# A graph layer's last places, its last blocks of nodes and its normalization, arranged differently

## The chip, the core and the metric

The kernel runs on one core of a Trainium2 chip. A core has five engines with instruction streams of their own: TensorE (PE in the profile; its weight loads are PEld), VectorE (DVE), ScalarE (ACT), GpSimd (POOL) and SyncE (SP), which here only issues DMAs. They wait for one another through semaphores, and each works its own instructions off in order. Sixteen DMA engines move data between the device memory and the on-chip memory. The metric is the time of one execution on the device, in microseconds (us).

## The reference

A message-passing layer over 12,500 nodes with 128 features and 400,000 edges sorted by destination, followed by a layer normalization over the features:

```
rbf      = exp(-(distances[:, None] - centers)**2 / (2 * width * width))      # 50 centers
cut      = 0.5 * (cos(pi * distances / 10) + 1) * (distances <= 10)
W        = (silu(rbf @ fw1 + fb1) @ fw2 + fb2) * cut[:, None]
messages = (h[src] @ pw + pb) * W
agg      = segment_sum(messages, dst, num_segments=num_atoms)
h_new    = h + (silu(agg @ mw1 + mb1) @ mw2 + mb2)
out      = layernorm(x + h_new)                                               # h is x
```

Edges longer than 10 have a factor of zero. The lengths are drawn so that 71,145 of the 400,000 edges are kept.

## The kernel before

**Preparation.** The projection h @ pw + pb of all nodes is computed first and stored in device memory as `proj`, 12,500 rows of 512 bytes. The edge list is taken in five chunks. For each, `pack` throws out the long edges by shifts and predicated copies on VectorE, and writes what is left close together into `packed`, a list in device memory that is cleared to zero beforehand. One entry has the source node (14 bits), the destination (14 bits) and a bit 28 that is set for an edge and not for an empty place. `pack` then reads the packed list back (`two`, L405), takes the source out of it (`part`, L408), clips it to N - 1 (`f_src`, L411), and turns it through TensorE into `srci`, the row indices of the gathers (L421). The list has 141 x 512 = 72,192 places. Places that no edge fills are zero, so that their source is row 0; their factor `cut` is zero.

**The loop.** It goes over 141 quads (`NQ`), each of four times 128 places. `fetch(q + 3)` (L478) issues four gathers on GpSimd, each of 128 rows of `proj` into `got`; `got` has eight buffers. `first` and `tanh`/`silu` compute the inner layer for two quads together, `second` (L539) the outer one into `pu` on TensorE, `message` (L550) multiplies `pu` by `got` on VectorE, `place` (L555) builds one-hot matrices `hot` of the edges' destinations on VectorE, `sum_up` (L564) adds up on TensorE into `pa`, and `add` (L583) adds `pa` at a place read from a register into `aggT` on VectorE. `add(q - 1)` stands behind `message(q)` and `place(q + 1)`. The schedule is manual: each engine runs its instructions in the order in which the program has them.

**The nodes.** The rows of nodes are worked off in 25 blocks of four tiles of 128 (the last has two: 128 and 84 rows), named by their first tile: 0, 4, ... 96. `node_first` (L594) has two matmuls on TensorE out of `aggT` and a tanh on ScalarE, `node_silu` (L604) one operation on VectorE, `node_second` (L611) nine matmuls on TensorE, then on VectorE one addition of 2x and four `bn_stats`. `scales` (L623) takes the statistics of up to four blocks and works out the reciprocal root by Newton steps on tiny tiles on VectorE, 20 operations, twelve of them in the four steps. `normalize` (L652) has one ScalarE activation for each tile and a store on SyncE.

As destinations are sorted, a block can begin when the quads with its destinations have been added. The lines L698 to L706 give each block a quad at which it begins in the loop, three quads apart and behind a bound on the progress of the list (`done_to`); the loop is left when a block would begin at quad 139 or later. So blocks 0 to 84 are in the loop (84 begins at 136), and 88, 92 and 96 are left to `finish` behind the last add. `nodes(q)` (L708) is called at the head of each quad; it has at most one block to normalize, and the stage of the block whose turn it is. At quad 137 it issues the loads of x for all blocks that are left. `finish` (L671) runs the rest, takes all their statistics in one group, and normalizes.

Of the kernel before, what the change touches and what calls it, by code (L numbers as in the profile page):

```python
# [10 lines left out]
F32 = mybir.dt.float32  # L11
BF16 = mybir.dt.bfloat16
I32 = mybir.dt.int32
AF = mybir.ActivationFunctionType
OP = mybir.AluOpType
# [13 lines left out]
SB = 14  # L29
# [5 lines left out]
NC_ = len(QB) - 1  # L35
NQ = QB[-1]
# [9 lines left out]
def kernel(  # L46
# [37 lines left out]
    nc = tc.nc  # L84
    N, H = x.shape
# [14 lines left out]
    x_sb = {}  # L100

    def load_x(t0, name="x4", bufs=8):
        t = work.tile([P, 4, H], F32, name=name, bufs=bufs)
        node_dma(t0, t, x, False)
        x_sb[t0] = t
# [88 lines left out]
    for name in ("pb", "fb2", "mb1", "mb2"):  # L194
# [4 lines left out]
    iota_n = keep.tile([P, WS], F32, name="iota_n")  # L199
# [23 lines left out]
                            op0=OP.mult, op1=OP.mult)  # L223
# [33 lines left out]
    for c in range(NC_):  # L257
        nc.vector.tensor_scalar(lim[:, c:c + 1], part_f[:64], float(2 * QB[c] - DONE[1]), 0.0,
                                op0=OP.add, op1=OP.max)
# [33 lines left out]
    def pack(c):  # L293

        if c + 1 < NC_:
# [12 lines left out]
                                op0=OP.mult, op1=OP.add)  # L308
# [9 lines left out]
        else:  # L318
# [14 lines left out]
        nodes = rowed(I32, "nodes", bufs=2)  # L333
        nc.vector.scalar_tensor_tensor(nodes, rel, SB, r_src, op0=OP.logical_shift_left,
                                       op1=OP.bitwise_or)
        yield 0.7
        nc.vector.scalar_tensor_tensor(nodes, step, LB, nodes, op0=OP.logical_shift_left,
                                       op1=OP.bitwise_or)
        yield 0.7
        for b in range(bits):  # L340
            k = 1 << b
# [4 lines left out]
                                    op0=OP.logical_shift_left, op1=OP.arith_shift_right)  # L346
            yield 0.4
            m = go[:, k:n + k]
            if b < bits - 1:
# [3 lines left out]
                                               op1=OP.bitwise_and)  # L353
                yield 0.7
                nc.vector.copy_predicated(after[:, :n], m, nodes[:, k:n + k])  # L355
                nodes = after
            else:
# [8 lines left out]
                                op1=OP.bitwise_and)  # L366
        nc.vector.tensor_scalar(to, to, first, None, op0=OP.add)
        yield 0.4
        both = rowed(I32, "both", CAP)
        nc.vector.tensor_scalar(both, front, (1 << SB) - 1, SB, op0=OP.bitwise_and,  # L370
                                op1=OP.logical_shift_left)
# [4 lines left out]
                                op0=OP.is_lt, op1=OP.mult)  # L376
        line = work.tile([P, CAP, 2], I32, name="line", bufs=2)
        nc.vector.scalar_tensor_tensor(line[:, :, 0], both, 1 << 2 * SB, there,
                                       op0=OP.bitwise_or, op1=OP.bitwise_and)
# [11 lines left out]
        p0, np_ = 2 * QB[c], 2 * (QB[c + 1] - QB[c])  # L391
# [5 lines left out]
        def paired(dt, name):  # L397
# [6 lines left out]
        two = paired(I32, "two")  # L404
        nc.vector.tensor_tensor(two, pair[:np_, 0, ::2], pair[:np_, 1, ::2], OP.bitwise_or)  # L405
        yield 0.7
        part = paired(I32, "part")
        nc.vector.tensor_scalar(part, two, SB, (1 << SB) - 1, op0=OP.logical_shift_right,  # L408
                                op1=OP.bitwise_and)
        f_src = paired(F32, "f_src")  # L410
        nc.vector.tensor_scalar(f_src, part, float(N - 1), None, op0=OP.min)  # L411
        yield 0.4
        tp = bank("ms").rearrange("p (f j e) -> p f j e", f=4, j=2)

# [7 lines left out]
        part = paired(I32, "part")  # L422
# [152 lines left out]
    def base_of(q, ks=(0, 1)):  # L575
        for k in ks:
            _, v = nc.values_load_multi_w_load_instructions(  # L577
                base_i[0:1, 2 * q + k:2 * q + k + 1], engines=[mybir.EngineType.DVE],
                min_val=0, max_val=N - W,
                skip_runtime_bounds_check_because="bases are destinations, and at most N - W")  # L580
            bases[q, k] = v[0]

    def add(q):  # L583
        pa = pa_of.pop(q)
        for k in range(2):
            to = aggT[:, ds(bases.pop((q, k)), W)]
            nc.vector.tensor_add(to, to, pa[:, k * W:(k + 1) * W])  # L587
# [6 lines left out]
    def node_first(t0):  # L594

        n = sum(rows(t0))
        pz = bank("ms")
        nc.tensor.matmul(pz[:, :n], bias_b["mb1"][:, 0, :], ones_b[:, :n], start=True, stop=False)
        nc.tensor.matmul(pz[:, :n], mw1_sb, aggT[:, t0 * P:t0 * P + n], start=False, stop=True)  # L599
        t = work.tile([P, QE], F32, name="zt", tag="xT", bufs=3)  # L600
        nc.scalar.activation(t[:, :n], pz[:, :n], AF.Tanh, scale=0.5)  # L601
        z_of[t0] = pz, t

    def node_silu(t0):  # L604
        n = sum(rows(t0))
        pz, t = z_of.pop(t0)
        s = work.tile([P, QE], F32, name="zs", tag="hp", bufs=3)
        nc.vector.scalar_tensor_tensor(s[:, :n], t[:, :n], 1.0, pz[:, :n], op0=OP.add, op1=OP.mult)
        zs_of[t0] = s

    def node_second(t0, st, tag="pu"):  # L611

        r = rows(t0)
        y = x_sb[t0]
        py = bank(tag).rearrange("p (k f) -> p k f", k=4)
        rows_times(py, zs_of.pop(t0), late["mw2"], bias_b["mb2"], r)
        for a, c, m in alike(r):
            nc.vector.scalar_tensor_tensor(y[:m, a:a + c], y[:m, a:a + c], 2.0, py[:m, a:a + c],
                                           op0=OP.mult, op1=OP.add)
        for k, m in enumerate(r):  # L620
            nc.vector.bn_stats(st[:m, k, :], y[:m, k, :])

    def scales(st, n):  # L623


        def tmp(name, dt=F32):
            return work.tile([P, 16], dt, name=name, bufs=1)[:, :n]

        def sts(o, a, v, b, op0, op1):
            nc.vector.scalar_tensor_tensor(o, a, v, b, op0=op0, op1=op1)  # L630

        mean, dif, v = tmp("mean"), tmp("dif"), tmp("v")
        nc.vector.tensor_add(mean, st[:, :n, 1], st[:, :n, 4])
        nc.vector.tensor_sub(dif, st[:, :n, 1], st[:, :n, 4])
        sts(dif, dif, 0.25, dif, OP.mult, OP.mult)
        nc.vector.tensor_add(v, st[:, :n, 2], st[:, :n, 5])
        sts(v, v, 1.0 / H, dif, OP.mult, OP.add)
        nc.vector.tensor_scalar(v, v, LN_EPS, None, op0=OP.add)
        g_i, g, w = tmp("g_i", I32), tmp("g"), tmp("w")
        nc.vector.tensor_scalar(g_i, v.bitcast(I32), 1, None, op0=OP.logical_shift_right)  # L640
        nc.vector.tensor_scalar(g_i, g_i, -1.0, float(0x5f3759df), op0=OP.mult, op1=OP.add)
        r, by = (work.tile([P, 16], F32, name=k, bufs=2)[:, :n] for k in ("rs", "by"))
        a = g_i.bitcast(F32)
        for k in range(4):
            nc.vector.tensor_mul(g, a, a)
            sts(w, g, -0.5, v, OP.mult, OP.mult)
            sts(r, w, 1.5, a, OP.add, OP.mult)
            a = r
        sts(by, mean, -0.5, r, OP.mult, OP.mult)
        return r, by  # L650

    def normalize(t0, rs, by):  # L652
        y = x_sb.pop(t0)
        for k, m in enumerate(rows(t0)):
            nc.scalar.activation(y[:m, k, :], y[:m, k, :], AF.Identity, bias=by[:m, k:k + 1],  # L655
                                 scale=rs[:m, k:k + 1])
        node_dma(t0, y, out, True)

    ready = []
# [1 line left out]
    def scaled(group, st):  # L661

        rs, by = scales(st, sum(len(rows(t)) for t in group))
        ready.extend((t, rs[:, t - group[0]:], by[:, t - group[0]:]) for t in group)
# [3 lines left out]
        nc.vector.memset(st, 0.0)  # L668
        return st

    def finish(these):  # L671

        for t0 in these[:4]:
            if t0 not in x_sb:
                load_x(t0)
        node_first(these[0])
        node_silu(these[0])
        if len(these) > 1:
            node_first(these[1])
        for k, t0 in enumerate(these):  # L680
            if k + 4 < len(these):
                load_x(these[k + 4])
            if k % 4 == 0:
                st = statistics()
            if k + 2 < len(these):
                node_first(these[k + 2])
            if k + 1 < len(these):
                node_silu(these[k + 1])
            node_second(t0, st[:, k % 4 * 4:])
            if k % 4 == 3 or k + 1 == len(these):  # L690
                scaled(these[k // 4 * 4:k + 1], st)
            if ready and k + 1 < len(these):
                normalize(*ready.pop(0))
        while ready:
            normalize(*ready.pop(0))


    begin, at_q = {}, NODES  # L698
    for t0 in range(0, NT, 4):
        while done_to(2 * at_q - 2) < min((t0 + 4) * P, N) and at_q < NQ:  # L700
            at_q += 1
        if at_q + 2 >= NQ:
            break
        begin[t0] = at_q
        at_q += 3
    early = list(begin)  # L706

    def nodes(q):  # L708

        if ready:  # L710
            normalize(*ready.pop(0))
        for k, t0 in enumerate(early):
            if begin[t0] - 8 == q:
                load_x(t0)
            if begin[t0] == q:
                node_first(t0)
            if begin[t0] + 1 == q:
                node_silu(t0)
            if begin[t0] + 2 == q:
                if k % 4 == 0:  # L720
                    st_of[0] = statistics()
                node_second(t0, st_of[0][:, k % 4 * 4:], "ms")
                if k % 4 == 3 or k + 1 == len(early):
                    scaled(early[k // 4 * 4:k + 1], st_of[0])
        if q == NQ - 4:
            for t0 in range(0, NT, 4):
                if t0 not in begin:
                    load_x(t0)
# [88 lines left out]
    for q in range(NQ):  # L817
# [38 lines left out]
        elif not todo and total is None:  # L856
            total = nc.values_load(bad_i[0:1, 0:1], min_val=0, max_val=2 * E)
    base_of(NQ - 1)
    add(NQ - 1)
    finish([t0 for t0 in tiles if t0 not in begin])  # L860


    with tc.If(total > 0):
# [79 lines left out]
```

## Time and profile before

| | us |
|---|---|
| median of 3 runs (838.05 to 838.92) | 838.82 |
| the profiled execution | 841.75 |
| its span, first to last instruction | 840.0 |

| engine | busy us | share of the span | instructions |
|---|---|---|---|
| PE | 595.8 | 71% | 3356 |
| DVE | 681.6 | 81% | 1834 |
| POOL | 582.3 | 69% | 613 |
| ACT | 260.5 | 31% | 404 |

The mean clock granted to TensorE is 0.841 of full speed. The page's second part shows the span in 40 equal slices of 21 us, each digit a share in tenths:

```profile
PE   4792767777777667776666787786877787876862
...
DVE  7967899989999999899857888777767767867754
...
POOL 3045777777777777777777777777777777777730
PEclk9896788778877888778987799998998987998976
DMA  8994324332253323333233343722623524622461
```

The first three slices are the projection and the first chunk; from the fourth or fifth on the loop runs, and what follows the last quad fills the last slice and the end of the one before. A row of the groups or of the timeline gives the line in the kernel, the engine, the operation, the tile written and the tiles read, and in brackets how long the engine had been idle before it and what ended that.

### The profile page before, as it was taken

The page shows a single profiled execution, that of the slowest core. Times are in us where ns is not written, and L with a number is a line of the kernel's source. Part 1 is how long each engine was busy: PE and PEld are TensorE (multiplying, and loading weights), DVE is VectorE, ACT ScalarE, POOL GpSimd, SP SyncE. Part 2 cuts the span into 40 slices and gives each one's busy share as a digit, 9 for nine tenths or more (in the row PEclk, how much of TensorE's full clock was granted, in tenths as well). Part 3 has the DMA queues.
Part 4 walks back from the last instruction along what each step waited for, and adds up shares of the span by engine and source line. Part 5 has one row for each costly group of instructions (what it writes and reads, how often), then busy time and mean ns, then how long its engine had stood idle before and what let it go on. Part 6 is the DMA issues. An engine that isn't in the chain of part 4 may idle for free.

```text
span 840.0 us, 11366 instructions
## 1 busy us (share of the span) xinstructions
PE 595.8 (71%) x3356; PEld 453.6 (54%) x3356; DVE 681.6 (81%) x1834; ACT 260.5 (31%) x404; POOL 582.3 (69%) x613
## 2 busy tenths in 40 slices
PE   4792767777777667776666787786877787876862
PEld 4780556555655455555454565664655555655551
DVE  7967899989999999899857888777767767867754
ACT  2454322222211322232222223432434232522512
POOL 3045777777777777777777777777777777777730
PEclk9896788778877888778987799998998987998976
DMA  8994324332253323333233343722623524622461
GB/s 244 269 278 138 94 61 126 77 101 75 52 146 78 86 75 76 78 85 88 76 84 91 103 115 80 191 66 76 179 79 98 157 79 104 166 69 61 127 54 34
DMA packets 85700, 90.62 MB, mean 108 GB/s; under 512 B 13623, under 2 KB 64851, under 8 KB 85632
## 3 DMA queue, kind: packets, MB, share of 16 engines
q1 hardware_dynamic: 66464, 49.95, 21.1%
q0 software_dynamic: 18912, 39.77, 20.0%
q8 instruction: 28, 0.46, 0.2%
q14 instruction: 40, 0.33, 0.1%
q10 hardware_dynamic: 256, 0.11, 0.1%
HBM read 74.71 MB, written 15.07 MB: 107 GB/s over the span
## 4 chain that ended last, share of the span: by engine, by line
DVE 41%; PE 18%; DMA 12%; issue 12%; POOL 10%; DVEq 4%; ACT 2%; SPq 0%; POOLq 0%; ACTq 0%
POOL got L482 10%; DMA got<-proj,srci 9%; DVE hot L560 8%; DVE s L534 5%; DVE aggT L587 4%; DVE msg L552 4%; PE pa L569 4%; PE ph L521 3%; DVEq L577 3%; DVE r_d L360 3%; PE pu L546 3%; DVE nodes L351 2%; PE pa L242 2%; DVE go L345 2%; DMA x<-in_x_dram 2%
## 5 line engine op out<-in xcount | busy, mean ns | idle before, releaser
L482 POOL DMA_INDIRECT got<-proj,srci x564 | 558.0, 989 | 171.9 <-issue 142.9
L569 PE MATMUL pa<-hot,msg 128*128 128x128 f32 x1128 | 182.5, 313 | 109.8 <-DVE msg L552 109.6
L569 PEld LDWEIGHTS pa<-hot,msg 128*128 128x128 f32 x1128 | 162.7, 222 | 123.5 <-DVE msg L552 122.8
L546 PEld LDWEIGHTS pu<-fw_h,s 128*128 128x128 f32 x1128 | 179.3, 226 | 11.6 <-issue 4.4
L546 PE MATMUL pu<-fw_h,s 128*128 128x128 f32 x1128 | 177.4, 309 | 0.0
L560 DVE TENSOR_SCALAR hot<-iota_n,dl,cut 128x128 f32<-128x128 f32 x564 | 157.9, 354 | 1.7 <-PE pa L569 1.1
L527 ACT ACTIVATE t<-ph 128x1024 f32<-128x1024 f32 (+1 forms) x71 | 71.9, 1013 | 267.7 <-PE ph L521 243.6
L521 PE MATMUL ph<-rbf,w_sb 51*128 51x512 f32 x282 | 106.6, 827 | 63.4 <-DVE s L534 54.1
L552 DVE TENSOR_TENSOR msg<-pu,got 128x512 f32<-128x512 f32 x141 | 96.5, 684 | 67.0 <-DMA got<-proj,srci 57.7
L534 DVE SCALAR_TENSOR_TENSOR s<-t,ph 128x1024 f32<-128x1024 f32 (+1 forms) x71 | 85.7, 1207 | 6.6 <-ACT t L527 6.6
L587 DVE TENSOR_TENSOR aggT<-aggT,pa 128x128 f32 x282 | 80.0, 284 | 7.5 <-PE ms L599 1.6
L521 PEld LDWEIGHTS ph<-rbf,w_sb 51*128 51x128 f32 x282 | 28.4, 228 | 84.9 <-issue 55.6
L543 PE MATMUL pu<-fb_b,ones_b 96*128 96x512 bf16 x141 | 62.8, 445 | 0.0
L601 ACT ACTIVATE zt<-ms 128x512 f32<-128x512 f32 (+1 forms) x25 | 14.7, 587 | 150.4 <-PE ms L599 150.4
L655 ACT ACTIVATE x<-x,by,rs 128x128 f32<-128x128 f32 x98 | 39.9, 482 | 68.0 <-DVE by L630 68.0
L511 ACT ACTIVATE rbf<-d,rbf_bias,rbf_scale 128x512 f32<-128x512 f32 (+1 forms) x71 | 57.1, 804 | 0.7 <-DMA d<-near_d 0.7
L543 PEld LDWEIGHTS <-ones_b 96*128 96x128 bf16 x141 | 14.6, 104 | 77.9 <-issue 77.4
L512 ACT ACTIVATE rbf<-rbf 128x512 f32<-128x512 f32 (+1 forms) x71 | 44.7, 630 | 2.2
L351 DVE SCALAR_TENSOR_TENSOR nodes<-go,nodes 128x625 int32<-128x625 int32 x45 | 36.4, 810 | 1.3
L360 DVE COPY_PREDICATED r_d<-go,r_d 128x624 int32<-128x624 int32 (+9 forms) x50 | 36.9, 738 | 0.0
L355 DVE COPY_PREDICATED nodes<-go,nodes 128x624 int32<-128x624 int32 (+8 forms) x45 | 35.9, 798 | 1.1
L382 POOL DMA_INDIRECT packed<-line,at_i x5 | 5.3, 1057 | 42.2 <-DVE first L300 41.0
(155 smaller groups left out, 516.4 us busy)
## 6 DMA issues: line engine op xcount, KB each, us to landing
d<-near_d SPq DMA_DIRECT2D x137, 128.0 KB, 3.5
x<-in_x_dram SPq DMA_DIRECT2D x48, 256.0 KB, 4.2
got<-proj,srci POOLq DMA_INDIRECT x564
proj<-hp SPq DMA_DIRECT2D x24, 256.0 KB, 4.7
out_dram<-x SPq DMA_DIRECT2D x24, 256.0 KB, 2.9
r_d<-in_edge_weight_dram SPq DMA_DIRECT2D x5, 312.5 KB
r_dst<-in_dst_dram SPq DMA_DIRECT2D x5, 312.5 KB
r_src<-in_src_dram SPq DMA_DIRECT2D x5, 312.5 KB, 6.4
```

The lines of the kernel that those rows point to most:

```text
L360: nc.vector.copy_predicated(r_d[:, :n], m, r_d[:, k:n + k])
L482: nc.gpsimd.indirect_dma_start(out=got[:, j, :], out_offset=None, in_=proj, in_offset=bass.IndirectOffsetOnAxis(ap=i, axis=0))
L511: nc.scalar.activation(rbf[:u], d[:u], AF.Square, bias=rbf_bias[:u], scale=rbf_scale[:u])
L521: nc.tensor.matmul(ph[:, h, :], w1_sb[p0:p0 + KR], rbf[p0:p0 + KR], start=True, stop=True)
L527: nc.scalar.activation(t[:, :n], ph[:, :n], AF.Tanh, scale=0.5)
L534: nc.vector.scalar_tensor_tensor(s[:, :n], t_of.pop(o)[:, :n], 1.0, ph[:, :n], op0=OP.add, op1=OP.mult)
L543: nc.tensor.matmul(pu, ones_b[:, :P], bias_b["fb2"].rearrange("k j f -> k (j f)"), start=True, stop=False)
L546: nc.tensor.matmul(pu[:, j * H:(j + 1) * H], s[:, j * P:(j + 1) * P], fw2_h, start=False, stop=(j == QT - 1))
L552: nc.vector.tensor_mul(msg, pu_of.pop(q).rearrange("p (j f) -> p j f", j=QT), got_of.pop(q))
L560: nc.vector.tensor_scalar(hot[:, j, :], iota_n[:, :W], dl[:, at[0], at[1]], cut[:, at[0], at[1]], op0=OP.is_equal, op1=OP.mult)
L569: nc.tensor.matmul(pa[:, k * W:(k + 1) * W], msg[:, j, :], hot[:, j, :], start=(j % 2 == 0), stop=(j % 2 == 1))
L587: nc.vector.tensor_add(to, to, pa[:, k * W:(k + 1) * W])
```

## The change

Four edits.

1. In the last chunk `pack` adds to the source of each empty place (bit 28 not set) its position in its row of 256, 0 to 255, before the clipping. That is one `scalar_tensor_tensor` and one `tensor_add` on 64 x 256 elements on VectorE.
2. One more block may begin in the loop, if its last stage falls behind the last quad. By the rule of L698 this is block 88, which begins at quad 139; 92 and 96 stay for `finish`. A new call `nodes(NQ)` stands between the register loads of the last add and the last add. The block has a statistics tile of its own and shares it with 92 and 96; `finish` gets it as `have` and `st` and scales all three together.
3. Three Newton steps instead of four.
4. In the last loop of `finish`, the first tile of a block is normalized on ScalarE and the others on VectorE.

```diff
--- before.py
+++ after.py
@@ -408,7 +408,15 @@
         nc.vector.tensor_scalar(part, two, SB, (1 << SB) - 1, op0=OP.logical_shift_right,
                                 op1=OP.bitwise_and)
         f_src = paired(F32, "f_src")
-        nc.vector.tensor_scalar(f_src, part, float(N - 1), None, op0=OP.min)
+        if c == NC_ - 1:
+
+            spread = paired(F32, "f_cut")
+            nc.vector.scalar_tensor_tensor(spread, two, float(1 << 2 * SB), iota_n[:np_, :256],
+                                           op0=OP.is_lt, op1=OP.mult)
+            nc.vector.tensor_add(f_src, part, spread)
+            nc.vector.tensor_scalar(f_src, f_src, float(N - 1), None, op0=OP.min)
+        else:
+            nc.vector.tensor_scalar(f_src, part, float(N - 1), None, op0=OP.min)
         yield 0.4
         tp = bank("ms").rearrange("p (f j e) -> p f j e", f=4, j=2)
 
@@ -641,7 +649,7 @@
         nc.vector.tensor_scalar(g_i, g_i, -1.0, float(0x5f3759df), op0=OP.mult, op1=OP.add)
         r, by = (work.tile([P, 16], F32, name=k, bufs=2)[:, :n] for k in ("rs", "by"))
         a = g_i.bitcast(F32)
-        for k in range(4):
+        for k in range(3):
             nc.vector.tensor_mul(g, a, a)
             sts(w, g, -0.5, v, OP.mult, OP.mult)
             sts(r, w, 1.5, a, OP.add, OP.mult)
@@ -649,11 +657,16 @@
         sts(by, mean, -0.5, r, OP.mult, OP.mult)
         return r, by
 
-    def normalize(t0, rs, by):
+    def normalize(t0, rs, by, both=False):
+
         y = x_sb.pop(t0)
         for k, m in enumerate(rows(t0)):
-            nc.scalar.activation(y[:m, k, :], y[:m, k, :], AF.Identity, bias=by[:m, k:k + 1],
-                                 scale=rs[:m, k:k + 1])
+            if both and k:
+                nc.vector.tensor_scalar(y[:m, k, :], y[:m, k, :], rs[:m, k:k + 1], by[:m, k:k + 1],
+                                        op0=OP.mult, op1=OP.add)
+            else:
+                nc.scalar.activation(y[:m, k, :], y[:m, k, :], AF.Identity, bias=by[:m, k:k + 1],
+                                     scale=rs[:m, k:k + 1])
         node_dma(t0, y, out, True)
 
     ready = []
@@ -668,7 +681,7 @@
         nc.vector.memset(st, 0.0)
         return st
 
-    def finish(these):
+    def finish(these, st=None, have=()):
 
         for t0 in these[:4]:
             if t0 not in x_sb:
@@ -677,39 +690,43 @@
         node_silu(these[0])
         if len(these) > 1:
             node_first(these[1])
-        for k, t0 in enumerate(these):
-            if k + 4 < len(these):
-                load_x(these[k + 4])
+        every = list(have) + these
+        for k, t0 in enumerate(every):
+            if t0 in have:
+                continue
+            if k + 4 < len(every) and every[k + 4] not in x_sb:
+                load_x(every[k + 4])
             if k % 4 == 0:
                 st = statistics()
-            if k + 2 < len(these):
-                node_first(these[k + 2])
-            if k + 1 < len(these):
-                node_silu(these[k + 1])
+            if k + 2 < len(every):
+                node_first(every[k + 2])
+            if k + 1 < len(every):
+                node_silu(every[k + 1])
             node_second(t0, st[:, k % 4 * 4:])
-            if k % 4 == 3 or k + 1 == len(these):
-                scaled(these[k // 4 * 4:k + 1], st)
-            if ready and k + 1 < len(these):
+            if k % 4 == 3 or k + 1 == len(every):
+                scaled(every[k // 4 * 4:k + 1], st)
+            if ready and k + 1 < len(every):
                 normalize(*ready.pop(0))
         while ready:
-            normalize(*ready.pop(0))
+            normalize(*ready.pop(0), both=True)
 
 
     begin, at_q = {}, NODES
     for t0 in range(0, NT, 4):
         while done_to(2 * at_q - 2) < min((t0 + 4) * P, N) and at_q < NQ:
             at_q += 1
-        if at_q + 2 >= NQ:
+        if at_q + 2 > NQ:
             break
         begin[t0] = at_q
         at_q += 3
-    early = list(begin)
+    last = [t0 for t0 in begin if begin[t0] + 2 == NQ]
+    early = [t0 for t0 in begin if t0 not in last]
 
     def nodes(q):
 
         if ready:
             normalize(*ready.pop(0))
-        for k, t0 in enumerate(early):
+        for k, t0 in enumerate(early + last):
             if begin[t0] - 8 == q:
                 load_x(t0)
             if begin[t0] == q:
@@ -717,10 +734,10 @@
             if begin[t0] + 1 == q:
                 node_silu(t0)
             if begin[t0] + 2 == q:
-                if k % 4 == 0:
+                if k % 4 == 0 or t0 in last:
                     st_of[0] = statistics()
-                node_second(t0, st_of[0][:, k % 4 * 4:], "ms")
-                if k % 4 == 3 or k + 1 == len(early):
+                node_second(t0, st_of[0][:, k % 4 * 4 if t0 in early else 0:], "ms")
+                if t0 in early and (k % 4 == 3 or k + 1 == len(early)):
                     scaled(early[k // 4 * 4:k + 1], st_of[0])
         if q == NQ - 4:
             for t0 in range(0, NT, 4):
@@ -856,8 +873,9 @@
         elif not todo and total is None:
             total = nc.values_load(bad_i[0:1, 0:1], min_val=0, max_val=2 * E)
     base_of(NQ - 1)
+    nodes(NQ)
     add(NQ - 1)
-    finish([t0 for t0 in tiles if t0 not in begin])
+    finish([t0 for t0 in tiles if t0 not in begin], st_of[0], last)
 
 
     with tc.If(total > 0):
```

## The prediction

> **What bounds the kernel now.** I read the page first (parts 2 and 5), then GpSimd's waits, then the order of time from 785 us on, and at last stretches of that end with their clock and DMA share. In the page's fifth part this row is the longest:
>
> ```profile
> L482 POOL DMA_INDIRECT got<-proj,srci x564 | 558.0, 989 | 171.9 <-issue 142.9
> ```
>
> 564 gathers keep GpSimd busy 558.0 us, and its idle 171.9 us are almost wholly 564 pauses of 0.30 us. So GpSimd issues one gather every 1.25 us, a quad (512 edges) every 5.0 us, from 73 us to the last at 807.08, and never waits for another engine for longer than that pause. VectorE has slack: in 37 quads it waits for got. **The loop is bound by the issue of gathers; nothing that is made faster inside it moves 807.08.** The change can only gain in the 33 us after it. They read so, in order of time (start, us, engine, what, idle before it and its releaser):
>
> ```profile
> 802.57 0.69 DVE L618 SCALAR_TENSOR_TENSOR x<-x,ms 128x512 f32<-128x512 f32 x1 [4.83 <-PE ms L242]
> ...
> 807.08 0.94 POOL L482 DMA_INDIRECT got<-proj,srci  x1 [0.30 <-issue]
> ...
> 808.34 0.69 DVE L552 TENSOR_TENSOR msg<-pu,got 128x512 f32<-128x512 f32 x1
> ...
> 809.08 2.08 PE L569 MATMUL pa<-hot,msg 128*128 128x128 f32 x8 [5.44 <-DVE msg L552]
> ...
> 814.49 0.69 DVE L552 TENSOR_TENSOR msg<-pu,got 128x512 f32<-128x512 f32 x1 [1.17 <-DMA got<-proj,srci]
> ...
> 816.75 0.61 DVE L587 TENSOR_TENSOR aggT<-aggT,pa 128x128 f32 x2 [0.68 <-PE ms L598]
> ...
> 830.04 3.95 ACT L655 ACTIVATE x<-x,by,rs 128x128 f32<-128x128 f32 x10 [9.02 <-DVE by L630]
> 831.72 3.30 SPq L121 DMA_DIRECT2D out_dram<-x  x4
> ```
>
> The messages at 808.34 and 814.49 are those of quads 138 and 140. The last gather lands only some 7.3 us after its start; in ten or more earlier quads where VectorE waited for got it was 2.6 to 2.8 us. The last message waits 1.17 us for it. The last add ends at 817.37 (T below), the last statistics at 825.95, the small operations at 830.01, the last activation at 833.99, the last issue at 835.02. The span is 840.0 and the profiled execution 841.75; these last 6.7 us I leave alone. The runs shown have a median of 838.82, 2.9 us lower; I sum against the profiled execution and carry the difference over.
>
> **Part 1, rows of their own for empty places.** The inputs keep 71,145 edges in 72,192 places, so the 1,047 empty ones are quads 139 and 140 and a little of 138; all fetch row 0. The stretches (clock, DMA share, GB/s at the end of a row) show its price:
>
> ```profile
> 765.00:767.50 2.50, 2.50 (x22) 2.37 (x22) 1.90 (x7) 0.39 (x1) 1.89 (x3) 1.00 0.22 54
> 803.40:808.10 4.70, 0.24 (x3) 0.05 (x1) 4.09 (x24) 0.00 (x0) 3.71 (x4) 1.00 0.81 36
> ```
>
> Gathers of mixed rows take 22% of the DMA engines for 54 GB/s, those of row 0 81% for 36: per byte over five times as long. Spread out, got(140) should land at 807.08 + 2.7 = 809.8 instead of 814.3. But VectorE ends the add of quad 138 only at 813.3: taken alone, this gains the 1.17 us of waiting, and more only if VectorE comes earlier. Cost: two operations on 64x256, like L411 (0.285 us) and L281 (0.417): 0.7 us on VectorE near 446 us, beside quads that wait for got (1.6 and 2.4 us there). [...] The gathers beside L280 and L281 took 1.07 and 1.09 us instead of 0.94: by the row 0.3 at most. I take 0.2.
>
> **Part 2, three Newton steps.** Each group of tiles loses three operations, one every 0.20 us: 0.6 us. Five groups lie under the gathers: nothing. The sixth (804.20 to 808.33) stands ahead of the message of quad 138: 0.6. The last stands ahead of the normalization: 0.6.
>
> **Part 3, block 88 begins in the loop.** Its start quad comes out as 139, so: first matmuls and tanh at 139, silu at 140, second matmul, sum and statistics behind quad 140 but *ahead of the last add*. On TensorE the first matmuls stand before second(140); the add of quad 138 must wait until they have read aggT; on ScalarE the tanh stands between the normalizations of tiles 80 and 84, of which only the stores are later. Behind silu(88) on VectorE waits message(140). The load of x moves on SyncE from quad 137 to 131, past the last near_d issues, where x has eight buffers; it leaves the burst at 787.55, four issues, three.
>
> The sum, with the 0.6 of part 2: message(138) 807.73, TensorE restarts at 808.47 at half clock. Sums(138) 1.9 → 810.35; first(88), as at 776.25 to 778.21, just under 1.96 → 812.2; second(140) 1.28 at full clock → 813.5; sums(139) 0.95 → 814.4. VectorE: add(138) 812.3 to 812.95, silu(88) → 813.65, message(140) → 814.35. Sums(140) → 815.45; second(88) 1.25 → 816.7; x and statistics 0.7 + 0.9 → 818.3; last add 0.6: **T = 818.95 instead of 817.37, 1.6 later.** Then finish has two blocks: first matmul and tanh of 92 to T + 1.9, silu T + 2.6, second matmul T + 3.65, x and statistics 1.55, those of block 96 0.95: T + 6.15, where the trace has T + 8.61. **The move by itself gains 2.5 and loses over 2.**
>
> [...]
>
> ```profile
> 795.00:798.00 3.00, 2.86 (x6) 1.30 (x7) 2.71 (x8) 0.60 (x1) 2.39 (x3) 0.50 0.30 71
> 798.00:801.00 3.00, 3.00 (x16) 2.94 (x16) 0.00 (x0) 0.00 (x0) 2.09 (x4) 0.50 0.29 44
> 801.00:804.00 3.00, 2.64 (x19) 2.32 (x17) 1.40 (x5) 0.00 (x0) 2.39 (x3) 0.90 0.75 44
> ```
>
> In the rows the clock is halved from 794.65 to 801.6, and again from 808.4 to 815.25: two lots of 6.8 us, in which TensorE was busy from 0.5 and 0.7 us after the start on. From 770.95 to 777.65 it was idle until 774.38, busy from there, and had its clock back 3.3 us later. [...] By the two long rows it stays halved to 815.25: second(140) → 814.7, sums(139) → 816.0, sums(140) → 817.0, T = 820.5. [...]
>
> **Part 4, VectorE normalizes too.** Before: ten activations at 0.395 each, then the last two issues, 830.01 to 835.02 = 5.0. After: three on ScalarE (1.2), seven on VectorE at the pitch of L560 (four in 1.11, two scalars per partition too): 2.0, and SyncE's last two issues (0.81 + 0.37, as now) behind: 3.3. Gain 1.7. Should the shared tile x make the two engines take turns, 0.5 of it goes.
>
> **Sum.** 818.95 + 6.15 = 825.1; 17 operations 3.45 → 828.55; + 3.3 → 831.85 instead of 835.02: −3.2, and 0.2 for GpSimd is within its rounding. 841.75 − 3.2 = 838.55; at the median 838.82 − 3.2 = **835.6 us**.
>
> **The rivals.**
> - [...]
> - *Half clock to 815.25*: T = 820.5, −1.6: 837.2, about no change.
> - *Spreading does nothing* (row 0 wasn't the cause): message(140) at 814.5 instead of 813.65, −2.5: 836.3. The share of 81% speaks against it.
> - *Slower: the last add behind block 88.* VectorE works in order, so the add waits for second(88), x and statistics. At half clock all through: sums(140) → 818.4, second(88) → 821.1, statistics → 822.7, T = 823.3, and the finish 2.0 longer: 838.2 for the last issue, +3.2: 842.0. It decides from T = 822.1 on (12.9 us from T to the last issue). For it: two long halved stretches. Against: TensorE would be busy nearly all the time from 808.47.
>
> **How the numbers follow.** Forecast 0.40, earlier chain 0.25, half clock to 815.25 0.20, no effect of spreading 0.06, slower 0.09. What a measurement can tell from no change is 0.2%, 1.7 us, so faster begins below 837.1: forecast, earlier chain, the third rival and a part of the half-clock case: 0.75; within: 0.16; slower 0.09. The range takes in the earlier chain with a microsecond below it and the half-clock case with one above: 832.3 to 838.3.
>
> **What would show it.** Gathers still 1.25 us apart to about 807; the last landing within 3 us and the DMA share near 0.2; seventeen small operations per group; the last add after the statistics of block 88, 10 us before the last `by`-operation at most; last activation-like work 2 us after it. I am wrong if the last add ends after 822, if the last gather starts over 1 us later, or if the stores' end doesn't follow the last normalization.

## The result, and the profile after

| | us |
|---|---|
| changed kernel, median of 7 runs (830.76 to 834.95) | 832.21 |
| kernel before on the same chip, median of 7 runs (837.28 to 839.61) | 838.64 |
| ratio, 95% interval | 0.9929 (0.9910 to 0.9948) |
| profiled execution of the changed kernel, its span | 830.76, 829.0 |

The change makes the kernel faster, by 6.4 us between the medians and by 6.0 by the ratio (4.4 to 7.5). I had forecast 3.2. 832.21 lies 0.1 below the low end of the range (832.3), which was set against a median of before of 838.82; on that median the ratio gives 832.9.

The two profiled executions differ by 11.0 us, and most of that isn't the change's. The profile of the changed kernel is its fastest run, that of before (841.75) lies above all seven runs of the table. Up to quad 60 both programs issue the same instructions, and yet the first gather of quad 60 already starts 5.4 us earlier; from quad 67 to the last gather the difference only goes from 5.0 to 5.2. The last gathers stand at 807.08 and 801.92, so that all else, 5.8 us, lies behind the last gather. I therefore read everything from there on as a distance from the *start of the last gather*, called G.

In the groups of the page the bound is as before: 564 pauses of about 0.30 us, busy time and mean of one nearly the same.

```profile
L490 POOL DMA_INDIRECT got<-proj,srci x564 | 553.8, 982 | 171.9 <-issue 146.6
```

The end of the changed kernel in order of time (start, us, engine, what, idle before it and its releaser), the lines that answer to those of before:

```profile
795.22 0.69 DVE L626 SCALAR_TENSOR_TENSOR x<-x,ms 128x512 f32<-128x512 f32 x1 [3.39 <-PE ms L242]
...
800.29 0.69 DVE L560 TENSOR_TENSOR msg<-pu,got 128x512 f32<-128x512 f32 x1
...
801.03 2.08 PE L577 MATMUL pa<-hot,msg 128*128 128x128 f32 x8 [4.74 <-DVE msg L560]
...
801.92 0.94 POOL L490 DMA_INDIRECT got<-proj,srci  x1 [0.30 <-issue]
...
805.97 0.68 DVE L560 TENSOR_TENSOR msg<-pu,got 128x512 f32<-128x512 f32 x1
...
809.01 0.69 DVE L626 SCALAR_TENSOR_TENSOR x<-x,ms 128x512 f32<-128x512 f32 x1 [0.87 <-PE ms L242]
...
810.53 0.59 DVE L595 TENSOR_TENSOR aggT<-aggT,pa 128x128 f32 x2
...
820.82 1.26 ACT L668 ACTIVATE x<-x,by,rs 128x128 f32<-128x128 f32 x3 [7.59 <-DVE by L638]
820.82 1.88 DVE L665 TENSOR_SCALAR x<-x,rs,by 128x128 f32<-128x128 f32 x7
```

The message of quad 140 (805.97) has no wait in brackets: got was there before VectorE was. The last add (810.53) stands behind the operation and the statistics of block 88, as the program has it. And the first line, the operation on block 84, is 6.7 us ahead of G, where before had it 4.5 ahead. Set against the steps of the forecast, all in us from G:

| step | before | forecast | after | off |
|---|---|---|---|---|
| operation on block 84 starts | −4.5 | −4.5 | −6.7 | −2.2 |
| message(138) starts | 1.3 | 0.65 | −1.6 | −2.3 |
| message(140) starts | 7.4 | 6.6 | 4.05 | −2.5 |
| last add ends | 10.3 | 11.9 | 9.2 | −2.7 |
| last small operations start | 18.9 | 18.0 | 15.45 | −2.6 |
| they end | 22.9 | 21.5 | 18.9 | −2.6 |
| last store is issued | 27.9 | 24.8 | 22.1 | −2.7 |
| span ends | 32.9 | 29.8 | 27.1 | −2.7 |

Nearly the whole miss is there at the first row, before the last gather even starts. Everything behind it went as summed, to half a microsecond.

### The profile page after: what moved, and what is told of

Same layout as the page of the kernel before. It is cut to its first block, busy times and chain, and to the rows that moved or that the text cites. A ratio compares the mean times of both kernels' runs of the same rounds, so it can differ in the third digit from the quotient of the medians.

```text
span 829.0 us, 11346 instructions
## 1 busy us (share of the span) xinstructions
PE 588.0 (71%) x3356; PEld 449.8 (54%) x3356; DVE 679.6 (82%) x1822; ACT 257.6 (31%) x397; POOL 578.6 (70%) x613
## 4 chain that ended last, share of the span: by engine, by line
DVE 33%; POOL 17%; PE 16%; DMA 15%; issue 14%; DVEq 3%; ACT 1%; SPq 1%; POOLq 0%; ACTq 0%
POOL got L490 16%; DMA got<-proj,srci 11%; DVE hot L568 8%; DVE s L542 4%; PE pa L577 4%; DVE msg L560 3%; DVE aggT L595 3%; PE ph L529 3%; PE pu L554 3%; DMA x<-in_x_dram 3%; DVEq L585 2%; DVE r_d L360 2%; PE pa L242 1%; PE ms L242 1%; DVE st L629 1%
## 5 line engine op out<-in xcount | busy, mean ns | idle before, releaser
L577 PE MATMUL pa<-hot,msg 128*128 128x128 f32 x1128 | 184.6, 315 | 107.1 <-DVE msg L560 106.8
L554 PEld LDWEIGHTS pu<-fw_h,s 128*128 128x128 f32 x1128 | 176.2, 223 | 12.0 <-issue 5.1
L554 PE MATMUL pu<-fw_h,s 128*128 128x128 f32 x1128 | 174.8, 306 | 0.0
L529 PE MATMUL ph<-rbf,w_sb 51*128 51x512 f32 x282 | 101.3, 791 | 63.9 <-DVE s L542 53.3
L668 ACT ACTIVATE x<-x,by,rs 128x128 f32<-128x128 f32 x91 | 37.3, 482 | 59.4 <-DVE by L638 59.4
L626 DVE SCALAR_TENSOR_TENSOR x<-x,ms 128x512 f32<-128x512 f32 x23 | 15.8, 686 | 24.9 <-PE ms L242 24.9
```

What stands on the lines that cost most here:

```text
L529: nc.tensor.matmul(ph[:, h, :], w1_sb[p0:p0 + KR], rbf[p0:p0 + KR], start=True, stop=True)
L554: nc.tensor.matmul(pu[:, j * H:(j + 1) * H], s[:, j * P:(j + 1) * P], fw2_h, start=False, stop=(j == QT - 1))
L577: nc.tensor.matmul(pa[:, k * W:(k + 1) * W], msg[:, j, :], hot[:, j, :], start=(j % 2 == 0), stop=(j % 2 == 1))
```

## The experiments

Each kernel ran with the kernel before on the same chip. The first four ran on one chip, on which the kernel before had a median of 839.0 (29 runs). The changed kernel did not run again with them, so the comparisons with it go by its ratio to before and by the distances from G.

### Part 1 undone, and part 1 alone

```diff
 # no_spread: the changed kernel without
-        if c == NC_ - 1:
-            spread = paired(F32, "f_cut")
...
+        nc.vector.tensor_scalar(f_src, part, float(N - 1), None, op0=OP.min)
```

> The changed kernel with part 1 undone: empty places fetch row 0 again. In the changed kernel's profile message(140) starts 4.05 us after the start of the last gather and doesn't wait for it. Theory 'landing' (the rival of the earlier chain: VectorE reaches message(140) before rows of place 0 would have landed): the last gather lands some 7.3 us after its start, message(140) waits for it 3.3 us later than in the changed kernel, and 27.1 us from the start of the last gather to the end of the span become 30.4; time 835.5. Theory 'chain' (my forecast: TensorE and VectorE reach message(140) that late anyway): message(140) doesn't move, 27.1 to 27.4, 832.2 to 832.5.

Measured: 836.83, ratio 0.9981 (0.9963 to 0.9998). The order of time of this kernel:

```profile
797.60 0.69 DVE L618 SCALAR_TENSOR_TENSOR x<-x,ms 128x512 f32<-128x512 f32 x1 [5.00 <-PE ms L242]
...
802.68 0.94 POOL L482 DMA_INDIRECT got<-proj,srci  x1 [0.30 <-issue]
...
810.31 0.69 DVE L552 TENSOR_TENSOR msg<-pu,got 128x512 f32<-128x512 f32 x1 [1.80 <-DMA got<-proj,srci]
```

Message(140) waits for got again and starts 7.6 after G; the span ends 30.7 after G instead of 27.1. These 3.6 us are those by which message(140) comes later. Between the ratio of this kernel and that of the changed one lies 0.52%, 4.4 us, and their intervals don't touch. The time is 1.3 us over the 835.5 of the theory 'landing', and further from that of the theory 'chain'.

The other way round, only_spread is the kernel before with these lines of the change and nothing else.

> The kernel before with part 1 alone. The kernel before has 32.9 us from the start of the last gather to the end of the span. Theory 'landing': message(140) no longer waits, and starts when VectorE has ended add(138); with the operation on block 84 4.5 us before the start of the last gather, as in the profile of before, that gains 1.2 us, with it 6.7 us before, as in the profile of the changed kernel, 3.4: 29.5 to 31.7, 835.2 to 837.4. Theory 'chain': 1.2 at most whatever the place of block 84, 31.7, 837.4. That row 0 isn't what slows the last gather: it lands 7 us after its start still, 838.6.

Measured: 835.34, ratio 0.9953 (0.9929 to 0.9976), by the ratio 3.9 us less than before (2.0 to 6.0), which leaves out the 1.2 of the theory 'chain'. In its order of time:

```profile
797.08 0.69 DVE L626 SCALAR_TENSOR_TENSOR x<-x,ms 128x512 f32<-128x512 f32 x1 [1.68 <-PE ms L242]
...
805.44 0.94 POOL L490 DMA_INDIRECT got<-proj,srci  x1 [0.30 <-issue]
...
808.19 0.69 DVE L560 TENSOR_TENSOR msg<-pu,got 128x512 f32<-128x512 f32 x1 [0.35 <-DMA got<-proj,srci]
```

Here VectorE came early enough to see the last landing itself: 2.75 after G instead of 7.4. The span ends 28.3 after G, 4.7 less than before and less than the 29.5 expected at best, since block 84 came earlier than in either profile that the expectation was made from (8.4 us ahead of G). That settles both halves of part 1: the identical row was what made the last gathers slow, and their landing, not the engines' chain, was what message(140) waited for, in all three profiles with the identical row (before, no_spread, and only_block below). The stretches (length, busy times of PE, PEld, DVE, ACT and POOL, clock, DMA share, GB/s) of the changed kernel's last gathers show the price gone, 20% for 51 GB/s where before had 81% for 36:

```profile
797.90:801.90 4.00, 0.87 (x4) 0.87 (x5) 3.61 (x17) 1.59 (x4) 2.83 (x3) 0.84 0.20 51
```

### Block 88 undone, and block 88 alone

```diff
 # no_block: the changed kernel with
-        if at_q + 2 > NQ:
+        if at_q + 2 >= NQ:
 # only_block: the changed kernel without part 1, and with
-        for k in range(3):
+        for k in range(4):
...
-            normalize(*ready.pop(0), both=True)
+            normalize(*ready.pop(0))
```

> The changed kernel with part 2 of its text undone: block 88 is left to the end again (spread rows, three Newton steps and both engines for the normalization stay). By my sum from rows the last add then ends 6.5 us after the start of the last gather instead of 9.2, and 15.3 us of finish follow instead of 12.9: 26.8 from the start of the last gather to the end of the span instead of 27.1. Theory 'the block is worth nothing': 831.9 to 832.8, the upper end if the burst of four loads of x makes got(136) and with it block 84 later. Theory 'the block pays': its 2.4 us shorter finish isn't given back, 29 us and 834.5.

> The kernel before with block 88 in the loop alone (row 0, four Newton steps, ScalarE alone). Theory 'the block is worth nothing': message(140) still waits for the last gather, 7.4 us after its start, the add of quad 140 stands behind block 88, and 27.1 + 3.35 + 1.2 + 1.8 = 33.4 us follow the start of the last gather, where before has 32.9: 839.1. Theory 'the block pays': some 2 us less than before, 30.9 and 836.6.

Measured: no_block 833.38, ratio 0.9935 (0.9911 to 0.9959); only_block 840.46, ratio 1.0012 (0.9999 to 1.0026). Both times lie above what 'the block is worth nothing' expected, by 0.6 and 1.4 us. That of no_block can't rule out the 834.5 of 'the block pays', which is within its interval of 2 us to either side; that of only_block is 3.9 us from the 836.6. From G to the end of the span: 27.0 and 32.6 us, against 27.1 of the changed kernel and 32.9 of before; expected were 26.8 and 33.4, or 29 and 30.9 if the block pays. The block is worth nothing that shows, as the sum had it. What it gives back stands in only_block's order of time: message(140) waits for its landing, and the last add stands behind the operation and the statistics of block 88, 1.5 us after that operation's start,

```profile
809.52 0.69 DVE L552 TENSOR_TENSOR msg<-pu,got 128x512 f32<-128x512 f32 x1 [2.37 <-DMA got<-proj,srci]
...
812.57 0.69 DVE L618 SCALAR_TENSOR_TENSOR x<-x,ms 128x512 f32<-128x512 f32 x1 [0.52 <-PE ms L242]
813.29 0.87 DVE L621 BATCH_NORM_STATS2 st<-x 128x6 f32<-128x128 f32 x4
814.08 0.59 DVE L587 TENSOR_TENSOR aggT<-aggT,pa 128x128 f32 x2
```

whereas in no_block the last add comes right when its sums are there, and ends 6.5 after G (expected 6.5) instead of 9.2:

```profile
808.46 0.61 DVE L595 TENSOR_TENSOR aggT<-aggT,pa 128x128 f32 x2 [0.69 <-PE ms L606]
```

### The same profiles, read for the clock

For the place of block 84 I had a cause in mind, the burst of x loads at quad 137 (with four loads got(136) lands late, and TensorE comes late by it), and a doubt, where in time the changes of TensorE's clock fall. In before and after the clock goes between full and half (1.00 and 0.50), and its changes (89 and 77) all lie whole multiples of 3.41 us apart, from 3.41 to 47.8 us; a stretch of 3.41 us of this grid is called a window here. All 84 times that it was halved, TensorE had been busy for 1.97 us or less of the window ahead of that. Six profiles speak on block 84. The clock's changes in them are read from stretches of 0.4 us:

| kernel | loads of x at quad 137 | message(136) after its last gather | clock halved ahead of block 84, from G | block 84 from G |
|---|---|---|---|---|
| before | 4 | 4.6 | −12.3 to −5.5 | −4.5 |
| no_spread | 3 | 3.8 | −12.4 to −5.6 | −5.1 |
| no_block | 4 | 4.1 | −11.2 to −7.8 | −6.4 |
| after | 3 | 4.0 | −11.6 to −8.1 | −6.7 |
| only_block | 3 | 3.6 | −11.2 to −7.8 | −6.9 |
| only_spread | 4 | 3.9 | not halved | −8.4 |

In only_spread message(136) waited for TensorE, in the others for got. The order of the last column is that of the length for which the clock was halved: 6.8, 3.4 or 0 us. It isn't that of the loads: four loads stand at both ends. So the burst is refuted as what decides, though it may still cost tenths. The stretches of two kernels, first before, then after:

```profile
794.77:798.18 3.41, 3.04 (x7) 1.48 (x8) 2.94 (x9) 0.60 (x1) 2.66 (x3) 0.50 0.26 63
798.18:801.59 3.41, 3.41 (x17) 3.26 (x17) 0.00 (x0) 0.00 (x0) 2.64 (x3) 0.50 0.30 43
```

```profile
790.36:793.78 3.42, 3.42 (x16) 3.33 (x16) 1.44 (x6) 0.60 (x1) 2.55 (x3) 0.50 0.21 53
793.78:797.20 3.42, 2.51 (x21) 2.24 (x19) 1.88 (x8) 0.00 (x0) 2.51 (x4) 1.00 0.14 43
```

In before the clock stays halved through two windows (6.8 us) and VectorE does nothing in the second (0.00), waiting for TensorE; in after it is back after one (3.4 us). What remains unsettled is why it was back after one window in one and not in the other: that the length of the halved stretch and the place of block 84 go together is shown; that the phase of the windows decides, where they fall in time, is not, since the kernel made to force the clock said nothing on it (next part).

### Four kernels on another chip

They ran on a chip on which the kernel before took 1140.83 us (34 runs). There engines stood still for up to 45 us at a time, by the waits of add_first with a releaser outside what the profile follows:

```profile
POOL got L490 <- DVE msg L560: 204.9, 33, 34.0
ACT t L535 <- remote: 186.8, 10, 44.8
```

So GpSimd waited for messages, its last gather was long done when message(140) came (29 to 31 us after its start in these kernels), and nothing that depends on the landing or on G could be tried. In all four profiles the clock was full ahead of block 84, with the added matmuls of warm and without. I tell what was meant, the ratios, and what a distance from message(140) on still says.

```diff
 # burst_back
-            if begin[t0] - 8 == q:
+            if begin[t0] - 8 == q and t0 not in last:
...
-                if t0 not in begin:
+                if t0 not in begin or t0 in last:
```

> The changed kernel with the load of x for block 88 moved back from quad 131 to quad 137, so that four loads stand together there again. In the profiles so far the operation on block 84 starts between 4.5 and 8.4 us before the start of the last gather; 8.4 in a kernel with four loads, 5.1 in one with three. Theory 'burst' (as my prediction had it: with four loads got(136) is late and so is TensorE): got(136) lands 0.6 us later than in the changed kernel (message 4.6 us after its last gather, not 4.0), block 84 is at 4.5, message(140) 2.2 us later: +2.2, 834.8. Theory 'phase' (where TensorE's clock window falls decides, whatever the burst): no difference of the times beyond their interval, 831.5 to 833.5, block 84 anywhere from 4.5 to 8.4.

Ratio 0.9950 (0.9915 to 0.9985). Inconclusive: message(136) did not wait for got there. That the burst doesn't decide rests on the table above.

```diff
 # warm
+    def busy(n, w=None):
+        w = bank("ms") if w is None else w
+        for _ in range(n):
+            nc.tensor.matmul(w, ones_b[:, :P], ..., start=True, stop=True)
+        return w
...
+        if q in (NQ - 5, NQ - 3):
+            w = busy(3 if q == NQ - 5 else 11)
         msg = message(q)
         sum_up(q, msg)
+        if q == NQ - 5:
+            busy(4, w)
```

> The changed kernel with 18 matmuls that nobody reads, of 0.38 us each, put into TensorE's idle times: seven about the message of quad 136 and eleven ahead of that of quad 138. Theory 'phase': TensorE has no window of idle time, the clock stays full through the last five quads, block 84 starts 8.4 us or more before the start of the last gather, message(140) is held only by its landing, 2.7 to 2.8 us after the start of the last gather instead of 4.05: 25.8 us from there to the end of the span instead of 27.1, and the times of this kernel scatter less than those of the changed one; 831.0. If the added matmuls get into the way of real ones instead: block 84 at 6 us or less, 832 to 834.

Ratio 0.9959 (0.9932 to 0.9987). Inconclusive, as the three others had the full clock ahead of block 84 too. Nor did the added matmuls do all they were for: the eleven took 2.54 us where 4.2 had been reckoned, TensorE then stood 2.3 us for message(138), its clock was halved from 1103.0 to 1106.4, and message(140) waited 0.65 us for it.

```diff
 # add_first
-    nodes(NQ)
     add(NQ - 1)
+    nodes(NQ)
```

> The changed kernel with the last add ahead of the last stage of block 88 instead of behind it. Theory 'order' (the add waits in VectorE's order for second(88), x and statistics, as the prediction's sum has it): the last add ends some 0.7 us behind sums(140), 6.7 instead of 9.2 us after the start of the last gather, the first matmul of block 92 follows directly behind second(88), and the end comes 2.2 us earlier: 24.9 instead of 27.1, 830.0. Theory 'filled anyway' (x and statistics of 88 only move into the way of block 92): 27, 832.

Ratio 0.9929 (0.9904 to 0.9954). Of the order it does speak:

```profile
1116.79 0.68 DVE L560 TENSOR_TENSOR msg<-pu,got 128x512 f32<-128x512 f32 x1
...
1118.94 0.61 DVE L595 TENSOR_TENSOR aggT<-aggT,pa 128x128 f32 x2 [0.70 <-PE pa L577]
...
1119.84 0.69 DVE L626 SCALAR_TENSOR_TENSOR x<-x,ms 128x512 f32<-128x512 f32 x1 [0.17 <-PE ms L242]
```

The add ends 2.8 us after message(140) instead of 5.15 (5.2 in warm, on the same chip, with the order of the change), and from message(140) to the last group of small operations are 9.1 us instead of 11.4 (11.4 in warm too): 2.3 us shorter, as 'order' expected. That the whole kernel is faster for it isn't shown: the changed kernel itself didn't run on that chip, and the intervals of burst_back and warm overlap this one.

```diff
 # both_moves: add_first, and
-                if t0 in early and (k % 4 == 3 or k + 1 == len(early)):
+                if t0 in early and k % 4 == 3:
...
+        if q == NQ - 1:
+            scaled(early[len(early) // 4 * 4:], st_of[0])
```

> As add_first, and the small operations for blocks 80 and 84 moved from quad 138 to the head of quad 140, into the time in which VectorE waits for the last gather. message(138) no longer waits 3.4 us for them. Theory 'landing': message(140) is then held by the landing alone, 2.7 to 2.8 us after the start of the last gather, whatever the clock did before: 1.3 less than add_first, 23.6 from there to the end of the span, 828.7. If the small operations are late (block 84 near 4.5): message(140) at 4 as before, and no gain over add_first.

Ratio 0.9895 (0.9861 to 0.9929), the lowest of all, with an interval that overlaps add_first's. That it is faster than add_first isn't shown; the medians of all their runs are 1132.5 and 1134.1 us. Where the landing is no bound the small operations are only moved, and TensorE's wait with them: they end at 1107.7, just ahead of message(140), and TensorE stood 4.03 us for that message and did block 88 at half clock (its eight matmuls of L242 took 1.81 us, in add_first 1.05):

```profile
1107.53 0.17 DVE L638 SCALAR_TENSOR_TENSOR by<-mean,rs 128x8 f32<-128x8 f32 x1
...
1108.21 0.68 DVE L560 TENSOR_TENSOR msg<-pu,got 128x512 f32<-128x512 f32 x1
...
1108.95 1.16 PE L577 MATMUL pa<-hot,msg 128*128 128x128 f32 x8 [4.03 <-DVE msg L560]
```

From message(140) to the last small operations are 10.8 us, longer than add_first's 9.1. Whether the move pays where the landing holds the last message, for which it was meant, stays open.

## Why the prediction was right and where it was wrong

**The bound: right.** Gathers 1.25 us apart to the end, and nothing of the change moved them: 0.2 us of difference from quad 67 on.

**Part 1: right in its mechanism, wrong in its size, and with it the whole: 3.2 us forecast, 6 measured.** The step that failed reads "taken alone, this gains the 1.17 us of waiting, and more only if VectorE comes earlier". Alone it gained 3.9 us, in the changed kernel 4.4, two thirds or more of the whole. The landing was sized well (2.75 after G against 2.7 forecast). The term off is the one I took as given: VectorE ready at 813.3, 6.2 after G. It came from one profiled execution in which the clock was halved for two windows (6.8 us) ahead of block 84; in four of the five other profiles of the table it was one window (3.4 us) or none. (How often it is which, six profiles can't say, and all but those of before and only_spread were of executions faster than their kernel's median.) In an execution with an early chain the wait for got in the kernel before was not 1.2 us but longer: only_block shows 2.4, no_spread 1.8 although its clock was halved for two windows. The waits hid the chain, so the times of before couldn't show whether it was faster in other executions than in the profile. The earlier chain, which has a chance of 0.25 in the prediction (VectorE comes earlier than in the profile of before, and the spread rows then pay in full), had this outcome: block 84 came 2.2 us earlier, and the end 5.8, both from G. That the range reached down to the result, or to within 0.1 us of it, is owed to this rival, which had set its lower end. The *cause* that I had in mind for it was wrong: not the burst. Message(136) came 0.6 us earlier after its last gather than in before (4.0 against 4.6), but kernels with the four loads had it just as early (3.9 and 4.1). The third rival of the chances, spreading without effect, was wrong too: only_spread gained 3.9 us.

**The two operations of part 1.** They took 0.41 and 0.42 us where 0.7 in all was estimated; the gathers beside them took 1.06 and 1.13 us, together 0.3 over the usual 0.94. Forecast was 0.2, and 0.3 at most by the row.

**Part 2: right.** The last group takes 3.42 us from its start to its end, 4.03 before; 3.45 was forecast.

**Part 3: right, within a microsecond or two.** "The move by itself gains 2.5 and loses over 2": 32.6 against 32.9 us from G without the other parts, 27.1 against 27.0 with them. Behind the last add the small operations start 6.25 us later, forecast 6.15.

**The clock.** The sum has TensorE restart at half clock at 808.47 and do second(140) at full clock from 812.2 on. That a return so early can be counted on no run shows. What they showed behind message(138): in after the clock fell at 800.6 and was back at 804.0, one window, with TensorE begun 0.4 us after the fall (2.99 of 3.42 us busy), and in no_block it was one window too, with the same 2.99; in only_block, in which TensorE began after 0.66 us (2.75 of 3.41 busy), it was two, as in before with the same 2.75. Ahead of block 84 it was two in no_spread, though TensorE was busy for the whole of the first, as its stretches below show, and two in before with 3.04 of 3.41 us in the first, more than the 2.99 that were behind message(138). (In before the clock fell at 794.77, by the finer stretches, and not at 794.65 as I had it, and TensorE began 0.4 us after that.) Between the first and the last change of the clock in before and in after, all 67 halved windows with 3.40 us or more of TensorE's time busy had the full clock behind them, and of the 22 with 2.94 to 3.36 us only 15. So it is not safe to take the clock as back behind a window that is busy by the trace. The slow windows of before and no_spread hold the two 512-column matmuls of `first`, the quick ones of after and no_block don't; whether that is the reason was not tried.

```profile
790.25:793.66 3.41, 3.41 (x11) 1.86 (x11) 2.31 (x8) 0.60 (x1) 2.77 (x3) 0.50 0.24 63
793.66:797.08 3.42, 3.42 (x17) 3.27 (x17) 0.00 (x0) 0.00 (x0) 2.54 (x3) 0.50 0.26 38
```

**Part 4: right.** From the last small operation to the last store's issue 3.2 us, forecast 3.3, before 5.0. The two engines didn't take turns on x: both start at 820.82. Parts 2 and 4 together were 2.9 in the forecast; no_spread, which has them and the block, is 1.6 us faster than before, and the block alone 1.0 slower, so that 2.6 are left for them, with intervals of over a microsecond to either side.

**The slower rival: no.** Its mechanism is real, the add does stand behind block 88 and pays 2.3 us for it (add_first), but the last add ended 9.2 after G; it would have decided from 15.0 on (822.1 against 807.08).

## What to carry to other kernels

When a wait ends an engine's idle time, the length of that wait tells only how late the *engine* was in this one execution; ask what else could have been ready, and size the gain of removing the transfer from the transfer (7.3 us against 2.7), with the idle time as the lower end. When an engine's chain passes through stretches of changing clock, take several profiles before its arrival is used as a fixed number (ahead of block 84 the clock was halved for 0, 3.4 or 6.8 us in six of them). And padding of a gather's index list deserves different rows: 1,047 empty places out of 72,192 cost 4 us of 839 at the end of the list.

## What had not been expected of the hardware

Gathers whose 128 places all name one and the same row of 512 bytes took over five times the DMA time per byte (81% of the engines for 36 GB/s, against 22% for 54), and the last of them landed 7.3 us after its start instead of 2.7. In no_spread a halved window in which TensorE was busy by the trace from end to end (3.41 of 3.41 us) had another halved one behind it. And one chip ran the kernel before in 1140.8 us instead of 839.0; in add_first, profiled there, engines waited up to 45 us for something that the profile doesn't name, while GpSimd's mean for a gather (979 ns) and VectorE's for a message (684 ns) were those of the other chip (982 and 683 ns in the changed kernel).
